# Joining the second graph's softmax totals with layer 0's totals in one 80-column product

## The chip, the cores and the metric

One core of a Trainium2 chip (trn2) runs the whole kernel in one launch. The metric is the device time of one execution in microseconds. Three runs of the kernel before are at hand; their median is what the changed kernel is held against. A separate execution was profiled, and every duration below comes from that one.

## The reference, cut to what matters

Sixty-four graphs of 256 nodes with 512 features pass through two graph layers, all in float32.

```python
# layer 0, for each graph: one attention of rank one, masked by adj
f = x @ fc_w.T + fc_b
logits = q(f) + k(f).T
a0 = softmax(leaky(logits + (1 - adj) * -1e9), axis=-1)
x1 = a0 @ f + x

# layer 1, for each graph: 8 heads of 64, weighted by adj
Q, K, V = x1 @ W_q + b_q, x1 @ W_k + b_k, x1 @ W_v + b_v
s = Q_h @ K_h.T / 8 + a[:, None] + c[None, :] + b_g + log(adj + 1e-9)
out = softmax(s, axis=-1) @ V_h + x1
```

Both softmaxes are computed without a maximum: the kernel forms the exponentials, uses them unnormalised in the products, and divides by their row totals later. The totals are what the change is about. `in_range` checks that no reciprocal of a total left a safe range; if one did, a general version at the end of the kernel would recompute everything.

## The kernel before, in words

The graphs are handled in 32 groups of two. The program is unrolled and its order is written out by hand: `step(d, a, f, n, check)` works on four groups at once. In step g, `f` is group g in its layer 0, `a` is group g-1 in its layer 1, `d` is group g-2, of which only the second graph's last part is left, and `n` is group g+1, whose inputs are being loaded. Short strings such as `D("attend:1 totals_1")` name the methods in the order in which they are issued; each engine's instructions are executed in that order. Step 0 has no `a`, steps 0 and 1 have no `d`, and the last step has no `n`, so it finishes group 30 by a tail of its own.

TensorE (PE) does the projections as seven block products each (`Product`, `Mixed`; L412), the scores `sc` (L843), the attention output `oT` (L883) and layer 0's mixing `y` (L667). VectorE (DVE) multiplies exponentials by the adjacency mask (`factor`, L863), adds them up (`both`, L870), and does the 32 x 32 transposes and the sums of block products. ScalarE (ACT) does the exponentials and copies out of PSUM.

A layer-1 total is made in four pieces. `parts` (L899, L900) transposes the summed exponentials in 32 x 32 blocks and reduces them, which leaves for each graph a tile `part` of 2 x 32 columns. `totals` (L910) multiplies it by `every`, a constant that adds over the four 32-row quarters of the partitions and spreads the sums; it does so in two products of 64 output partitions each, for even and odd heads. `ratios` (L925) takes reciprocals out of PSUM into `recip1`. `divide` (L983) multiplies the turned output `osb` by them, `complete` (L991) adds the residual and `store` sends it out.

Layer 0 has the same kind of total: `parts_0` (L613, L614) makes 16 columns in `part0`, `recip` (L621) multiplies them by `every`, four small ACT copies (L625) sort the result into `tot`, and a DVE reciprocal (L628) fills `recip0`.

The start of the step, where the change is, reads so before:

```python
A("scores:0")
D("attend:1 totals_1")
F("add_tiles")
A("scores:1 factor:0:0 factor:0:1 pv.sum_11 pv.p3 pv.p4")
D("ratios:1 turn:1")
F("parts_0")
A("factor:1:0 factor:1:1 pv.sum_10 both:0 both:1")
check()
F("mix:0 mix:1 ysum:0 recip")
D("divide:1 complete:1 store:1")
A("residual:1")
F("mix:2 mix:3 ysum:1 ysum:2 ysum:3")
```

`check()` does something in every fourth step only (steps 5, 9, 13, ... 29, and in 31): eight times it issues the six DVE instructions of `in_range` (L1030 to L1037). The second graph's totals of the group `d` were made ready (`parts:2`, `parts:3`) at the end of the step before.

Further on in the step, the features of layer 1 (`x`) are turned by DVE (`send`, L771), written to a DRAM buffer `xd` by the SP queue and read back turned (`fetch`, L789) as `x1T`. The third of four such pieces comes back by both the SP and the ACT queue (`fetch_by_both:0:1`). DVE's `xsum` (L375) forms block differences `t1b` of `x1T`, and PE's product `pq.p6` (`pq<-t1b,q_s`, L412) reads them.

PSUM has a pool of four banks that these products share (`bank`), and two pairs for the scores.

Of the kernel before, what the change touches and what calls it, by code (L numbers as in the profile page):

```python
# [10 lines left out]
F32 = mybir.dt.float32  # L11
I32 = mybir.dt.int32
AF = mybir.ActivationFunctionType
ALU = mybir.AluOpType
AX = mybir.AxisListType
ENGINES = {getattr(mybir.EngineType, e) for e in ("PE", "DVE", "Activation", "Pool", "SP")}

P = 128
# [7 lines left out]
def kernel(  # L26
# [64 lines left out]
    nc = tc.nc  # L91
    NB, N, D = x.shape
    NH = 8
    HD = D // NH
    B = 32
    RS = P // 4
    NC = D // P
# [3 lines left out]
    TOK = GP * N  # L101
# [14 lines left out]
            name=nc.get_next_instruction_name(), act_func_set_id=both[0], ins=[], outs=[]  # L116
# [43 lines left out]
    NR = 4  # L160
    recip0 = const.tile([P, NG, T], F32, tag="recip0", name="recip0")
    recip1 = const.tile([P, NR, GP, NC, N // B], F32, tag="recip1", name="recip1")

    def fast():
        main = ExitStack()
        with main:
            one = main.enter_context(tc.tile_pool(name="one", bufs=1))
            wts = main.enter_context(tc.tile_pool(name="wts", bufs=1))
            two = main.enter_context(tc.tile_pool(name="two", bufs=2))
# [9 lines left out]
            def bank(name):  # L179
                return ps.tile([P, 512], F32, tag="bank", name=name)  # L180
# [36 lines left out]
            every = const.tile([P, P], F32, tag="every", name="every")  # L217
            for q in range(P // B):
                for n in range(P // B):
                    rows = slice(q * B, (q + 1) * B)  # L220
# [299 lines left out]

            v_all = one.tile([P, T, D], F32, tag="v", name="v")

            class Group:


                def __init__(self, g):
                    self.g = g
# [80 lines left out]

                def parts_0(self):

                    turned = two.tile([P, TOK], F32, tag="xt", name=f"es0t_{self.g}")
                    self.part0 = one.tile([P, TOK // B], F32, tag="part0", name=f"part0_{self.g}")
                    nc.vector.transpose(turned, self.es0)  # L613
                    nc.vector.tensor_reduce(  # L614
                        self.part0, turned.rearrange("p (m c) -> p m c", c=B), AX.X, ALU.add
                    )

                def recip(self):

                    pt = bank(f"rc_{self.g}")[:, 0 : TOK // B]  # L620
                    nc.tensor.matmul(pt, lhsT=every, rhs=self.part0, start=True, stop=True)  # L621
                    tot = one.tile([P, T], F32, tag="tot0", name=f"tot0_{self.g}")
                    for q in range(P // B):
                        rows = slice(q * B, (q + 1) * B)
                        nc.scalar.copy(  # L625
                            tot[rows, :], pt[rows, :].rearrange("p (t q) -> p q t", q=P // B)[:, q]
                        )
                    nc.vector.reciprocal(recip0[:, self.g, :], tot)  # L628
# [263 lines left out]
                def parts(self, u):  # L892

                    g, (gr, hg), nb = self.g, divmod(u, 2), NC * N // B
                    if hg == 0:
                        self.part = two.tile([P, 2, nb], F32, tag="part", name=f"part_{g}_{gr}")
                    pool, tag = ((two, "osb"), (one, "e0"), (one, "e0"), (one, "adj"))[u]
                    turned = pool.tile([P, NC * N], F32, tag=tag, name=f"est_{g}_{u}")
                    nc.vector.transpose(turned, self.esum[u].rearrange("p a b i -> p (a b i)"))  # L899
                    nc.vector.tensor_reduce(  # L900
                        self.part[:, hg, :], turned.rearrange("p (m c) -> p m c", c=B),
                        AX.X, ALU.add,
                    )
# [19 lines left out]
                def ratios(self, gr):  # L923
                    self.rs = recip1[:, self.g % NR, gr]
                    nc.vector.reciprocal(self.rs.rearrange("p m b -> p (m b)"), self.tot)  # L925

                def sums_1(self, gr):

# [111 lines left out]
            def attention_and_layer_0(D, A, F, X, check):  # L1040

                A("scores:0")
                D("attend:1 totals_1")
                F("add_tiles")
                A("scores:1 factor:0:0 factor:0:1 pv.sum_11 pv.p3 pv.p4")
                D("ratios:1 turn:1")
                F("parts_0")
                A("factor:1:0 factor:1:1 pv.sum_10 both:0 both:1")
                check()
                F("mix:0 mix:1 ysum:0 recip")  # L1050
                D("divide:1 complete:1 store:1")
                A("residual:1")
                F("mix:2 mix:3 ysum:1 ysum:2 ysum:3")
                A("parts:0")
                F("pf.p1 pf.keep_1 pf.p2 pf.p6 pf.sum_00 begin send:0:0 fetch:0:0")
                A("turn_residual:1 parts:1")
                F("pf.p7 pf.p5")
                A("scores:2 attend:0 totals_0")
                F("pf.sum_11 send:1:1 fetch:1:1")
                A("factor:2:0 factor:2:1 turn:0")  # L1060
                F("pf.p3 pf.sum_01 send:0:1 pq.p1 pq.keep_1 copy:0 fetch_by_both:0:1")
                A("ratios:0 both:2")
                F("pf.p4 pf.sum_10 send:1:0")
                A("scores:3")
                F("fetch:1:0")
                A("factor:3:0")
                F("pk.p1 pk.keep_1 pv.p1 pv.keep_1")
# [16 lines left out]
            def step(d, a, f, n, check):  # L1084


                def of(group):
                    def issue(pieces):
                        for piece in pieces.split():
                            name, *args = piece.split(":")  # L1090
                            if group is None:
                                continue
                            target = group
                            if "." in name:
                                part, name = name.split(".")
                                target = getattr(group, part)
                            getattr(target, name)(*map(int, args))
                    return issue

                D, A, F, X = of(d), of(a), of(f), of(n)  # L1100
                X("load_adj")
                if a is not None:
                    attention_and_layer_0(D, A, F, X, check)
                else:
                    f.features_first()
                    F("pq.p1 pq.keep_1 copy:0 pk.p1 pk.keep_1 pv.p1 pv.keep_1")
                F("xsum:0 xsum:1 xsum:2 pq.p6 keys:2 keys:3 keys:0 keys:1")
                X("load_x")
                A("factor:3:1 both:3")
                F("pq.p7 pq.p2 pq.sum_00 xsum:3 pq.p5 pk.p6 pq.sum_11 pq.p3")  # L1110
                A("divide:0")
                X("dot_q:0 dot_q:1 dot_q:2 dot_q:3 spread")
                F("pq.p4 pq.sum_10 copy:1 copy:2")
                A("complete:0 store:0 parts:2")
                if n is None:
                    A("parts:3")
                F("pk.p7 pk.p5 pk.sum_11 residual:0")
                X("adjt")
                F("pk.p2 pk.sum_00")
                X("dot_k:0 dot_k:1")  # L1120
                F("pk.p3 pk.p4 pk.sum_10")
                X("dot_k:2 dot_k:3")
                F("turn_residual:0")
                if n is None:
                    A("attend:1 totals_1 ratios:1 turn:1 divide:1 complete:1 store:1")
                    F("residual:1 turn_residual:1")

                    F("pv.p2 scores:0 pv.p6 pv.sum_00 factor:0:0 factor:0:1 scores:1 both:0 pv.p7")
                    F("factor:1:0 factor:1:1 both:1 scores:2 pv.p5 sums_1:0 scores:3 pv.sum_11")
                    F("ratios_t:0 ratios_r:0 factor:2:0 factor:2:1 pv.p3 pv.p4 factor:3:0 pv.sum_10")  # L1130
                    F("factor:3:1 attend:0 finish:0 sums_of_e:1 attend:1")
                    F("ratios_t:1 ratios_r:1 finish:1")
                    check_ranges()()
                    return
                X("mask add_eps")
                F("pv.p2 pv.p6")
                X("weights:0")
                F("pv.p7 pv.p5")
                X("weights:1")
                F("pv.sum_00")  # L1140
                A("parts:3")

            with tc.manual_schedule(engines=ENGINES):
                f = Group(0)
# [8 lines left out]
                d, a, a_w = None, None, {}  # L1153
                for g in range(NG):
                    n = Group(g + 1) if g + 1 < NG else None

                    def check():

                        if d is not None and (d.g % NR == NR - 1 or d.g == NG - NR // 2 - 1):
                            in_range(d.g // NR * NR, d.g + 1, f"{d.g}")  # L1160
# [218 lines left out]
```

## Time and profile before

| what | value |
|---|---|
| median of 3 runs | 2327.16 us (2326.76 to 2327.59) |
| the profiled execution's own time | 2324.43 us |
| span of its first to its last instruction | 2322.6 us |
| PE busy | 2302.7 us, 99% of the span |
| DVE busy | 2092.7 us, 90% |
| ACT busy | 1071.0 us, 46% |
| granted TensorE clock, mean | 0.998 |

The profiled execution took 1.8 us more than its span and 2.7 us less than the median of the runs. A float32 product is carried out by PE in two passes, each with its own weight load (rows "PEld") and its own matmul record, so that the profile counts two or four records where the program has one or two products. The granted clock is full throughout, so durations of one row may be added.

### The profile page before, as it was taken

The numbers are of one execution on the slowest core, as the hardware profiler recorded it, in microseconds if no ns is written. First come the engines' busy times: TensorE is split into PE (matmuls) and PEld (weight loads), VectorE is DVE, ScalarE is ACT, GpSimd is POOL, SyncE is SP. The second block draws the span as 40 slices with busy tenths as digits, with TensorE's granted clock in tenths as the row PEclk, the third lists the DMA queues.
The fourth block names the chain that finished last, engine by engine and source line by source line (L and its number), as shares of the span: only waits on it lengthen the run. The fifth ranks groups of instructions, "written<-read, shape, count | busy, mean of one in ns | idle before, by whom it ended". The sixth has DMA issues, their size and how long they took to land.

```text
span 2322.6 us, 33706 instructions
## 1 busy us (share of the span) xinstructions
PE 2302.7 (99%) x12738; PEld 1906.0 (82%) x12738; DVE 2092.7 (90%) x3088; ACT 1071.0 (46%) x1865; POOL 122.0 (5%) x120
## 2 busy tenths in 40 slices
PE   9999999999999999999999999999999999999997
PEld 5888888888888888888888888888888888888885
DVE  6799889999899998999999999999999989999897
ACT  3544445444444444454444444444544445444443
POOL 0000000000000000000000000000000000000000
PEclk9999999999999999999999999999999999999999
DMA  4122323223322323232233223322222323323312
GB/s 132 48 59 72 78 75 67 64 66 84 79 73 56 68 73 78 73 69 60 69 80 84 64 61 67 80 78 73 64 60 73 78 74 68 64 64 85 79 46 38
DMA packets 517263, 163.84 MB, mean 71 GB/s; under 512 B 415188, under 2 KB 478696, under 8 KB 517096
## 3 DMA queue, kind: packets, MB, share of 16 engines
q1 hardware_dynamic: 505512, 156.25, 28.5%
q10 hardware_dynamic: 11584, 5.38, 0.8%
q8 instruction: 103, 1.69, 0.3%
q14 instruction: 64, 0.52, 0.1%
HBM read 95.43 MB, written 66.12 MB: 70 GB/s over the span
## 4 chain that ended last, share of the span: by engine, by line
PE 95%; DVE 2%; DMA 2%; issue 0%; ACT 0%; ACTq 0%; DVEq 0%
PE pv L412 17%; PE pq L412 16%; PE pk L412 16%; PE pf L412 16%; PE sc L843 10%; PE oT L883 10%; PE y L667 9%; DMA x1T<-xd 1%; DMA xd<-xt 1%; PE fp L696 1%; DVE t1b L375 0%; DMA fc_nat<-in_L_gnn_fc_w_dram 0%; PE tot L910 0%; DVE xt L771 0%; PE rc L621 0%
## 5 line engine op out<-in xcount | busy, mean ns | idle before, releaser
L863 DVE TENSOR_TENSOR e<-e,am 128x1024 f32<-128x1024 f32 x254 | 300.5, 1214 | 24.1 <-ACT e L857 24.1
L857 ACT ACTIVATE e<-sc,c 128x1024 f32<-128x1024 f32 x254 | 269.0, 1110 | 77.0 <-PE sc L843 73.5
L843 PE MATMUL sc<-qT,kT 64*128 64x256 f32 x2048 | 255.8, 389 | 0.4 <-ACT e L857 0.4
L883 PE MATMUL oT<-e,v 128*64 128x256 f32 x2032 | 233.4, 382 | 0.0
L495 POOL TENSOR_TENSOR pf_s<-pf_s,x 128x512 f32<-128x512 f32 x93 | 118.5, 1274 | 2118.7 <-ACT pf_s L494 1673.4
L843 PEld LDWEIGHTS sc<-qT,kT 64*128 64x128 f32 x2048 | 187.2, 186 | 51.5 <-issue 31.5
L667 PE MATMUL y<-e,x 128*128 128x256 f32 x992 | 226.1, 382 | 0.0
L883 PEld LDWEIGHTS oT<-e,v 128*64 128x64 f32 x2032 | 140.2, 137 | 85.4 <-issue 21.3
L432 ACT ACTIVATE pq_s<-pq,cols 128x256 f32<-128x256 f32 x192 | 80.5, 470 | 279.1 <-PE pq L412 279.1
L667 PEld LDWEIGHTS y<-e,x 128*128 128x128 f32 x992 | 186.1, 190 | 24.0
L494 ACT ACTIVATE pf_s<-pf,recip 128x256 f32<-128x256 f32 x186 | 77.9, 470 | 197.6 <-PE pf L412 197.6
L900 DVE TENSOR_REDUCE part<-est 128x32 f32<-128x1024 f32 x124 | 151.3, 1220 | 4.3
L899 DVE STREAM_TRANSPOSE est<-es 128x1024 f32<-128x1024 f32 x124 | 152.2, 1227 | 0.0
L870 DVE TENSOR_TENSOR es<-e,e 128x1024 f32<-128x1024 f32 x126 | 149.3, 1205 | 1.1
L673 ACT COPY yT<-y 128x512 f32<-128x512 f32 x124 | 72.6, 586 | 131.5 <-PE y L667 130.8
L890 ACT COPY oTs<-oT 128x512 f32<-128x512 f32 x128 | 75.0, 586 | 119.1 <-PE oT L883 98.4
L429 ACT COPY pk_s<-pk 128x512 f32<-128x512 f32 x96 | 56.3, 586 | 151.9 <-PE pk L412 151.9
L412 PE MATMUL pk<-x1T,wk 128*128 128x256 f32 x512 | 124.2, 385 | 0.0
L412 PE MATMUL pk<-t1b,wk 128*128 128x256 f32 x512 | 121.1, 379 | 0.4 <-DVE kT L443 0.4
L412 PE MATMUL pv<-wv,t1b_c 128*128 128x256 f32 x512 | 121.1, 379 | 0.0
L412 PE MATMUL pv<-wv,t1b 128*128 128x256 f32 x512 | 121.1, 379 | 0.0
L412 PE MATMUL pq<-x1T,wq 128*128 128x256 f32 x512 | 121.0, 379 | 0.0
(180 smaller groups left out, 4474.7 us busy)
## 6 DMA issues: line engine op xcount, KB each, us to landing
x<-in_x_dram SPq DMA_DIRECT2D x32, 1024.0 KB, 5.1
out_dram<-osb SPq DMA_DIRECT2D x254, 128.0 KB, 3.3
xd<-xt SPq DMA_DIRECT2D x124, 256.0 KB, 2.0
x1T<-xd SPq DMA_DIRECT2D x434, 64.0 KB, 1.9
adj<-in_adj_dram SPq DMA_DIRECT2D x128, 128.0 KB, 3.5
qrow<-q SPq DMA_DIRECT2D x31, 256.0 KB, 3.9
x1T<-xd ACTq DMA_DIRECT2D x62, 64.0 KB, 2.4
fc_nat<-in_L_gnn_fc_w_dram ACTq DMA_DIRECT2D x4, 256.0 KB, 3.8
```

What stands on the lines that cost most here:

```text
L412: nc.tensor.matmul(o, lhsT=lk[:, ts(m, P)] if len(lk.shape) == 2 else lk[:, m], rhs=rk, start=(start and m == 0 and k == 0), stop=(m == 1 ...
L432: nc.scalar.activation(dst[:, m], src[:, m], AF.Identity, bias=self.bias[:, 2 * o + m : 2 * o + m + 1],)
L494: nc.scalar.mul(s[:, m], src[:, m], self.recip[:, TPG * k + m : TPG * k + m + 1])
L495: nc.gpsimd.tensor_tensor(s, s, self.out(o, k), ALU.add)
L667: nc.tensor.matmul(y[:, ts(gr, N)], lhsT=self.x[:, gr * TPG + j, ts(c, P)], rhs=self.e0[:, j, gr, :], start=(gr == 0 and j == 0), stop=(gr ...
L843: nc.tensor.matmul(sc[:, par, pr, :], lhsT=self.kT[rows, 2 * hg + pr, ts(t, P)], rhs=self.qT[rows, 2 * hg + pr, ts(gr, N)], start=True, st ...
L857: nc.scalar.activation(e, sc, AF.Exp, bias=self.c[:, t : t + 1], scale=SCALE)
L863: nc.vector.tensor_tensor(ef, ef, self.am[:, jc, u // 2, :].unsqueeze(1).to_broadcast([P, 4, N]), ALU.mult,)
L870: nc.vector.tensor_tensor(self.esum[u], self.e[u, 0], self.e[u, 1], ALU.add)
L883: nc.tensor.matmul(oT[par * HD : (par + 1) * HD, pr, :], lhsT=self.v[:, gr * TPG + jc, ts(h, HD)], rhs=self.e[2 * gr + hg, jc][:, par, pr, :],
L899: nc.vector.transpose(turned, self.esum[u].rearrange("p a b i -> p (a b i)"))
L900: nc.vector.tensor_reduce(self.part[:, hg, :], turned.rearrange("p (m c) -> p m c", c=B), AX.X, ALU.add,)
```

## The change

`totals_1` and its two products of 2 x 16 columns are taken out of the step. `parts` now puts the second graph's 64 columns into the first part of a tile of 80 columns (`part_all`), and the younger group's `parts_0` writes layer 0's 16 columns behind them. `recip` multiplies all 80 columns by the full `every` in one product; its first 64 columns are handed to the older group (`all_sums`), the last 16 serve layer 0 as before. `ratios:1`, one reciprocal on 128 partitions, is replaced by `ratios_of_all`: two reciprocals on 64 partitions each, since even and odd heads now lie in different columns. It stands behind `recip`, just ahead of `divide:1`. `check()` moves behind `store:1`, so that it sees the new reciprocals. In step 1, which has no older group, `recip` keeps its 16 columns; the first graph's totals (`totals_0`, `ratios:0`) and the tail of the last step stay as they were.

```diff
+            ALL = 2 * NC * N // B + TOK // B
+
             class Group:
+                older = None
...
                     turned = two.tile([P, TOK], F32, tag="xt", name=f"es0t_{self.g}")
-                    self.part0 = one.tile([P, TOK // B], F32, tag="part0", name=f"part0_{self.g}")
+                    if self.older is None:
+                        self.parts_all = two.tile(
+                            [P, ALL], F32, tag="part", name=f"part0_{self.g}"
+                        )
+                    else:
+                        self.parts_all = self.older.part_all
                     nc.vector.transpose(turned, self.es0)
                     nc.vector.tensor_reduce(
-                        self.part0, turned.rearrange("p (m c) -> p m c", c=B), AX.X, ALU.add
+                        self.parts_all[:, ALL - TOK // B : ALL], turned.rearrange("p (m c) -> p m c", c=B), AX.X, ALU.add
                     )
...
-                    pt = bank(f"rc_{self.g}")[:, 0 : TOK // B]
-                    nc.tensor.matmul(pt, lhsT=every, rhs=self.part0, start=True, stop=True)
+                    lo = ALL - TOK // B
+                    first = lo if self.older is None else 0
+                    all_sums = bank(f"rc_{self.g}")[:, 0:ALL]
+                    nc.tensor.matmul(
+                        all_sums[:, first:ALL], lhsT=every, rhs=self.parts_all[:, first:ALL],
+                        start=True, stop=True,
+                    )
+                    if self.older is not None:
+                        self.older.all_sums = all_sums[:, 0:lo]
+                    pt = all_sums[:, lo:ALL]
...
-                        self.part = two.tile([P, 2, nb], F32, tag="part", name=f"part_{g}_{gr}")
+                        self.part_all = two.tile([P, ALL], F32, tag="part", name=f"part_{g}_{gr}")
+                        self.part = self.part_all[:, 0 : 2 * nb].rearrange("p (a m) -> p a m", a=2)
...
+                def ratios_of_all(self):
+                    self.rs = recip1[:, self.g % NR, 1]
+                    sums = self.all_sums.rearrange("p (a b m) -> p b a m", a=2, b=2)
+                    for par in range(2):
+                        rows = slice(par * HD, (par + 1) * HD)
+                        nc.vector.reciprocal(
+                            self.rs[rows].rearrange("p (a n) b -> p a (n b)", a=2), sums[rows, par]
+                        )
...
-                D("attend:1 totals_1")
+                D("attend:1")
...
-                D("ratios:1 turn:1")
+                D("turn:1")
                 F("parts_0")
                 A("factor:1:0 factor:1:1 pv.sum_10 both:0 both:1")
+                F("mix:0 mix:1 ysum:0 recip")
+                D("ratios_of_all divide:1 complete:1 store:1")
                 check()
-                F("mix:0 mix:1 ysum:0 recip")
-                D("divide:1 complete:1 store:1")
                 A("residual:1")
...
+                f.older = d
```

## The prediction

> **What bounds the kernel now.** I read the engines' shares first, then the chain that ended last, then PE's own waits.
>
> ```profile
> span 2322.6 us, 33706 instructions
> ...
> PE 2302.7 (99%) x12738; PEld 1906.0 (82%) x12738; DVE 2092.7 (90%) x3088; ACT 1071.0 (46%) x1865; POOL 122.0 (5%) x120
> ...
> PE 95%; DVE 2%; DMA 2%; issue 0%; ACT 0%; ACTq 0%; DVEq 0%
> ```
>
> PE's queue is the bound: 95% of the chain is PE after PE. So a step takes what PE's instructions take (71.16 us from one `rc` product to the next in 24 of the 30 intervals), and other engines count only where PE waits for them. PE's waits say where that is:
>
> ```profile
> PE pq L412 <- DVE t1b L375: 3.3, 6, 1.3
> ```
>
> Six waits, 3.34 us in all, and nothing else recurs. They are in steps 3, 4, 11, 18, 19 and 26, the intervals that are longer than 71.16 us. One of them, in time (start, length, instruction):
>
> ```profile
> 1327.75 0.69 DVE L375 TENSOR_TENSOR t1b<-x1T 128x512 f32<-128x512 f32 x1 [0.90 <-DMA x1T<-xd]
> 1328.47 0.69 DVE L375 TENSOR_TENSOR t1b<-x1T,t1b 128x512 f32<-128x512 f32 x1
> 1329.22 0.92 PE L412 MATMUL pq<-t1b,q_s 128*128 128x256 f32 x3 [0.35 <-DVE t1b L375]
> ```
>
> DVE waits for the third read-back of `x1T`, PE for DVE's second difference. In an ordinary step the first difference starts 26.93 us after `rc` and PE needs nothing before 28.89; as PE starts 0.06 us after the second difference ends (28.34), 0.49 us are spare.
>
> **What the Trainium skill says.** "TensorEngine Tiling (Array Packing)", Key Properties: changing the tiling mode drains TensorE. The trace agrees: from `pf` (whole array) to the scores (64 rows) the starts are 309 ns apart where whole-array passes are 216 ns apart. "TensorE: Matmul & The Clock Gate", LDWEIGHTS (loading the stationary operand): a load takes time by its columns, 128 / 1.2 = 107 ns; here back-to-back loads of 128 columns start 110 ns apart. "VectorE: DVE Perf Modes", Two Vector instructions with no wait between them: an instruction that starts in another quarter of the partitions than the one before is held until that has finished. The trace agrees: the four copies of L974 on different quarters start one duration plus 13 ns apart, while L925 and its successor overlap (332 ns long, 0.25 us from start to start). "Runtime: NRT & Kernel Launch", Instruction fetch mechanics: instructions come by DMA in blocks of 16 KiB, 256 of them. The trace has 103 such packets on queue 8, one for every 256 PE records, 0.9 to 1.9 us long.
>
> **PE: the removed product.** The second graph's totals in two steps, and the scores where they follow a plain product:
>
> ```profile
> 1219.54 0.26 PE L910 MATMUL tot<-part,every 128*64 128x32 f32 x4
> 1219.72 0.92 PE L843 MATMUL sc<-qT,kT 64*128 64x256 f32 x6
> ```
>
> ```profile
> 1169.16 0.81 PE L412 MATMUL pf<-fcT,tb 128*128 128x256 f32 x3
> 1169.90 0.70 PE L843 MATMUL sc<-qT,kT 64*128 64x256 f32 x4
> ```
>
> Record by record, the last `oT` pass before the totals starts at 1219.326, the first score at 1219.723: 209 + 35 + 152 = 396 ns. Without totals, `oT` (64 columns) meets the scores (64 rows) directly. No place in the steady steps shows this change of mode; its nearest rows are `pf` to `sc`, 309 ns, and the reverse `sc` to `oT`, 306 ns. The first pair of scores then takes 320 ns in both cases. I take 306: **90 ns saved in each of 30 steps (2 to 31), 2.7 us.** Bounds: at best the drain and the first pair's extra 104 ns vanish with the totals, 396 + 320 - 432 = 284 ns, 8.5 us; at worst the totals' slot is all drain anyhow and nothing is saved.
>
> **PE: the wider product.**
>
> ```profile
> 1228.66 0.29 PE L621 MATMUL rc<-part,every 128*128 128x16 f32 x2
> 1228.80 0.68 PE L667 MATMUL y<-e,x 128*128 128x256 f32 x2
> ```
>
> A pass of 256 columns takes 216 ns, 0.84 ns a column: 16 columns stream in 13 ns, 80 in 67 ns. But the two `rc` passes and the next `y` pass start their work 110 ns apart, as each waits for its weights, loaded while the pass before streams. 67 ns fit into 110. **Cost 0**; if the columns came on top, 64 x 0.84 x 2 = 108 ns a step, 3.2 us. Less than nothing is excluded: no weight load goes away here.
>
> **DVE.** One reciprocal of 332 ns leaves its old place ahead of `turn:1`. Nothing is gained: DVE then waits longer for `yT`. Two go in after the reciprocal of L628:
>
> ```profile
> 1300.64 0.69 DVE L350 TENSOR_TENSOR tb<-yT 128x512 f32<-128x512 f32 x1 [0.80 <-ACT yT L673]
> 1301.25 0.17 DVE L628 RECIPROCAL recip<-tot 128x4 f32<-128x4 f32 x1
> 1301.34 1.19 DVE L983 TENSOR_TENSOR osb<-osb,recip 128x1024 f32<-128x1024 f32 x1
> 1302.57 1.22 DVE L991 TENSOR_TENSOR osb<-osb,xb 128x1024 f32<-128x1024 f32 x1
> 1304.32 0.69 DVE L350 TENSOR_TENSOR tb<-yT,tb 128x512 f32<-128x512 f32 x1 [0.53 <-ACT yT L673]
> ```
>
> They lie on different quarters, so neither overlaps: 2 x 0.345 = 0.69 us (cover: the 0.53 us wait in the last line, which leaves 0.16 us). Behind are `ysum`, `parts:0`, the sums of `pf` and the sends on SP. The next wait of DVE, 0.90 us for POOL's `pf_s` ahead of the second sum of `pf`, swallows the rest. **Cost 0 in a step without a check.** The reciprocals add no wait either: L628, just ahead of them, already waits for ACT's copies of the same PSUM bank.
>
> **The moved check, eight steps.** Its six instructions take 1.62 us. Before, 0.80 us of that ran while DVE would have waited for `yT`, and the 0.53 us wait took most of the rest; the sum `ysum:1` came only 0.12 us late. Now the check stands after `complete`: `ysum:1` starts 0.16 + 1.62 = 1.78 us late, at 6.28 us after `rc`, and ends at 6.96; PE's `pf.p6` reads it as weights and starts at 7.13, with its 110 ns load this just fits. Then the delay goes down the queue: 1.78 - 0.90 (wait for POOL) = 0.88, less 0.14 idle ahead of the third sum: the third `send` is **0.74 us late**, and on SP and ACT its two-queue `fetch` behind it. `pf.p4`'s wait (0.50) and ACT's `e` (0.67) bring DVE itself back. The read-back then lands about 27.4 us after `rc` instead of 26.6; the first difference can start up to 27.42 before PE waits. Cost about 0 without a fetch of instructions in the way (between 0 and 0.3 us each, 0 to 1.8 us), and the whole 0.74 us where one makes the read-back late already.
>
> **Which steps these are.** All six waits are steps where a block of PE instructions comes in 22.8 to 25.6 us after `rc`, that is 282 to 318 records into the step (places counted in multiples of 256); 268 and 334 brought none. A step has 802 PE records, so the place moves back by 34 a step. The totals take 8 away, and perhaps a wait instruction: 793 or 794, a shift of 25 or 26. Counting on, blocks fall on 282 to 318 in steps 4, 5, 14, 15 (near its edge), 25 or 24, with 24 or 26 doubtful: about six again, so I leave their 3.34 us as they are (2 to 6 us possible). Steps 5 and 25 are check steps: **2 x 0.74 = 1.5 us lost.**
>
> **Other edits.** PSUM: a freed bank goes to the next tile in order of release. One tile less per step gives `y` of chunk 0 the bank of the first `oT`, long copied; the bank of `rc`, now freed by `ratios_of_all` (about 2.2 us after `rc`), goes to `pf.p2` at 5.4 us. Cover 3 us, cost 0. `parts` writes into a wider tile at the same durations (L900, 1220 ns). The `rc` product waits for `parts_0` as before; `parts:3` is done 11 us earlier. ACT, POOL and the stores keep their order; `store:1` comes 0.7 us later on SP in plain steps and SP then waits for `send` anyway.
>
> **Sum.** -2.7 + 0 + 0 + 1.5 = -1.2 us: 2324.4 becomes 2323.2 in the profiled execution. This stood 2.7 us under the median; held against the median, 2327.2 - 1.2 = **2326.0 us**.
>
> **Rivals.**
> A, *forecast*: PE saves its 90 ns and the checks give half back: 2322.4 to 2330.5. Chance 0.81, within 0.2% (4.7 us, about what a measurement of this kernel can tell from no change).
> B, *slower*: DVE's lateness reaches PE. If the third send is late by 0.74 us in all eight check steps and the read-back's margin is already used up, and the slower drift gives seven fetches at the price of steps 3 and 4 (1.0 us each on average): -2.7 + 8 x 0.74 + (7.2 - 3.3) = +7.1, 2334.3 us. It decides once the read-back lands later than 27.4 us in ordinary steps too. For it: 0.49 us spare is little. Against: waits of 0.90, 0.50 and 0.67 us lie between. Chance 0.12.
> C, *faster*: no drain between `oT` and the scores (284 ns a step, -8.5 us) and no loss at the checks: 2318.7 us. Against: `sc` to `oT` shows the drain. Chance 0.07.
> D, *it does not do what it says*: 80 columns stream on top, +3.2 us: 2329.2 us, inside the range and within A's chance.
>
> **Numbers.** The low end is A with no loss at the checks and two microseconds fewer of fetch waits (2322.4); the high end has D and one more fetch of instructions at step 4's price, 1.3 us (2330.5). Outside lie C and B.
>
> **What would show it.** Right: `oT` to `sc` starts about 306 ns apart, `rc` to `y` unchanged at 140 ns, L350's 0.53 us wait nearly gone, steps of 71.07 us, PE waits for `t1b` near 4 to 5 us in all, in steps 4, 5, 14, 15, 25. Wrong: waits of PE in most check steps, a new releaser in PE's waits, or `rc` to `y` longer by about 100 ns.

## The result, and the profile after

The changed kernel takes **2331.47 us** (median of 20 runs), the kernel before 2326.61 us (median of 20): a ratio of 1.0021, 95% interval 1.0015 to 1.0028, that is 4.9 us more. The forecast was 2326.0 us, within 0.2% of the kernel before, with a range that ended at 2330.5 us.

The shares and the chain of waits of the changed kernel (busy time, share of the span, instructions; then shares of the chain that ended last):

```profile
span 2329.5 us, 33496 instructions
...
PE 2304.3 (99%) x12618; PEld 1896.3 (81%) x12618; DVE 2114.3 (91%) x3118; ACT 1070.9 (46%) x1865; POOL 124.3 (5%) x120
...
PE 86%; DVE 8%; DMA 3%; issue 1%; ACT 0%; SPq 0%; ACTq 0%; POOL 0%; DVEq 0%
```

PE has 120 matmul records fewer, yet its part of the chain fell from 95% to 86%; DVE's rose from 2% to 8%. PE's waits (what waited, for what, us in total, times, longest):

```profile
PE pq L412 <- DVE t1b L375: 10.3, 12, 1.3
```

Before it was 3.3 us in six waits. Step by step, from one `rc` product to the next, the plain steps became shorter, from 71.162 to 71.075 us, and the steps with a check became longer, to 72.24 us (steps 9, 13, 17, 21 and 29, within 0.03 us of each other).

| where, profiled executions | us |
|---|---|
| 30 steps, each 87 ns shorter | -2.6 |
| the check steps 5 to 29, beyond 71.08 us | +8.7 |
| waits in other steps: 4.4 after, 5.0 before | -0.6 |
| start-up, until the first `rc` product | +1.3 |
| from the last `rc` product to the end | +0.1 |
| sum (spans: 2329.5 - 2322.6) | +6.9 |

The start-up is not of the change: with the same start the kernels below reach their first `rc` product between 87.4 and 91.0 us. The medians, 4.9 us apart, agree with the first three rows (+5.5) within a microsecond. The eighth check, in step 31, hides in the row before the last: PE waits 0.73 us there too and its last wait ends 1.0 us later, but what follows that wait took 6.8 us instead of 7.7. It takes 6.7 to 7.0 us in every run with the change and 7.8 in experiment 2, which is without it; the cause stays open.

This is check step 9 in the timeline, on DVE and POOL (start, length, instruction, idle time before it); `rc` starts at 659.29:

```profile
665.48 0.16 DVE L1068 TENSOR_TENSOR okp<-okp,okp 128x1 f32<-128x1 f32 x1
665.56 0.68 DVE L350 TENSOR_TENSOR tb<-yT,tb 128x512 f32<-128x512 f32 x1
666.16 1.76 DVE L350 TENSOR_TENSOR tb<-yT 128x512 f32<-128x512 f32 x1
667.85 0.68 DVE L350 TENSOR_TENSOR tb<-yT,tb 128x512 f32<-128x512 f32 x1
...
665.82 1.56 POOL L495 TENSOR_TENSOR pf_s<-pf_s,x 128x512 f32<-128x512 f32 x1 [62.90 <-ACT pf_s L494]
```

The check's last instruction is followed by the three `ysum`. The second of them takes 1.76 us where its neighbours take 0.68: it starts while POOL adds `x` to `pf_s`, and ends only after that. Before, POOL's add, at the same 6.5 us after `rc`, lay over a transpose and a reduction and met no such instruction. Check step 17 of the kernel before (DVE, then POOL; `rc` starts at 1228.66):

```profile
1235.09 1.24 DVE L899 STREAM_TRANSPOSE est<-es 128x1024 f32<-128x1024 f32 x1
...
1235.18 1.28 POOL L495 TENSOR_TENSOR pf_s<-pf_s,x 128x512 f32<-128x512 f32 x1 [62.98 <-DVE tb L350]
```

The rest of the way to PE, in step 9 of the changed kernel:

```profile
684.58 0.85 ACTq L808 DMA_DIRECT2D x1T<-xd  x2
685.48 2.12 ACT L876 ACTIVATE e<-sc,c 128x1024 f32<-128x1024 f32 x2 [3.01 <-PE sc L862]
686.62 1.23 DVE L882 TENSOR_TENSOR e<-e,am 128x1024 f32<-128x1024 f32 x1 [1.25 <-ACT e L876]
687.79 0.69 DVE L375 TENSOR_TENSOR t1b<-x1T 128x512 f32<-128x512 f32 x1
688.52 0.69 DVE L375 TENSOR_TENSOR t1b<-x1T,t1b 128x512 f32<-128x512 f32 x1
689.27 1.56 PE L412 MATMUL pq<-t1b,q_s 128*128 128x256 f32 x6 [0.88 <-DVE t1b L375]
```

The third send is late, so the ACT queue issues its half of the read-back late (25.30 us after `rc` instead of 23.74). Behind it in the same queue stand the exponentials of `scores:3`: they start at 26.2 us, though the last of these scores ended at 25.4. Behind these stands `factor:3:0`, and behind that, without idle time, the block differences, and PE.

### The profile page after: what moved, and what is told of

Same layout as the page of the kernel before. It is cut to its first block, busy times and chain, and to the rows that moved or that the text cites. A ratio compares the mean times of both kernels' runs of the same rounds, so it can differ in the third digit from the quotient of the medians.

```text
span 2329.5 us, 33496 instructions
## 1 busy us (share of the span) xinstructions
PE 2304.3 (99%) x12618; PEld 1896.3 (81%) x12618; DVE 2114.3 (91%) x3118; ACT 1070.9 (46%) x1865; POOL 124.3 (5%) x120
## 4 chain that ended last, share of the span: by engine, by line
PE 86%; DVE 8%; DMA 3%; issue 1%; ACT 0%; SPq 0%; ACTq 0%; POOL 0%; DVEq 0%
PE pv L412 16%; PE pq L412 16%; PE pk L412 16%; PE pf L412 12%; PE sc L862 9%; PE oT L902 8%; PE y L686 8%; DMA xd<-xt 2%; DMA x1T<-xd 1%; DVE x L501 1%; DVE est L919 1%; DVE xt L790 1%; DVE t1b L375 1%; DVE tb L350 1%; PE fp L715 1%
## 5 line engine op out<-in xcount | busy, mean ns | idle before, releaser
L412 PE MATMUL pq<-t1b,q_s 128*128 128x256 f32 x512 | 117.1, 382 | 10.4 <-DVE t1b L375 10.3
```

The source lines that it names most:

```text
L412: nc.tensor.matmul(o, lhsT=lk[:, ts(m, P)] if len(lk.shape) == 2 else lk[:, m], rhs=rk, start=(start and m == 0 and k == 0), stop=(m == 1 ...
```

## The experiments

**1. Without the checks.** 

> The changed kernel without the range checks inside the steps (left out: the check of all reciprocals but the last two groups'). Theory 1 (the moved check makes the third send late, and PE waits about 0.86 us in each of the eight check steps): those waits go, what is left is PE's 0.083 us a step and the fetch steps; about 2324 us, 2.5 to 3 us under the kernel before, and the interval of a check step without a fetch of instructions is 71.08 us. Theory 2 (the two held reciprocals or the joint product are what costs): the time stays near 2331 us.

```diff
                 D("ratios_of_all divide:1 complete:1 store:1")
-                check()
```

Measured 2322.8 us, ratio to before 0.9986 (0.9979 to 0.9992). The intervals of steps 9, 13, 17, 21 and 29 are 71.08 us. So the product and the two reciprocals save what they were to save; everything that made the change slower hangs on the check.

**2. The kernel before, with the check moved.** 

> The kernel before with the one edit that check() stands behind store:1; totals and reciprocals as they were. Theory 1: the loss of the changed kernel appears without its product: PE waits 0.7 to 0.9 us in each check step, 1.0 to 1.2 us longer intervals, about 2326.6 + 8 x 1.1 = 2335 us. Theory 2: no change, 2326 to 2327 us.

```diff
-                check()
                 F("mix:0 mix:1 ysum:0 recip")
                 D("divide:1 complete:1 store:1")
+                check()
```

Measured 2327.7 us, ratio 1.0006 (0.9998 to 1.0014): a miss for theory 1 as I had put it. The timeline of its step 9 (DVE, then POOL) shows why it is informative:

```profile
668.54 0.68 DVE L350 TENSOR_TENSOR tb<-yT 128x512 f32<-128x512 f32 x1
669.14 1.76 DVE L350 TENSOR_TENSOR tb<-yT,tb 128x512 f32<-128x512 f32 x1
...
668.94 1.40 POOL L495 TENSOR_TENSOR pf_s<-pf_s,x 128x512 f32<-128x512 f32 x1 [62.99 <-ACT pf_s L494]
```

The collision is here too, with the third `ysum` instead of the second, 1.08 us again. But without the two late reciprocals the whole queue is 0.76 us earlier: the first late `ysum` starts 5.51 us after `rc` instead of 6.27, and the third send ends at 22.35 instead of 23.23. That is just at the edge: PE's wait is 0.01 to 0.02 us in four check steps (intervals of 71.44 to 71.45 us, 0.28 more than a plain step), 0.09 in step 9 and 0.66 in step 13, where a block of instructions came at 19.7 us. Moved check and collision together cost little; the reciprocals' 0.7 us on top are what is too much.

Step 5 has no wait at all. Its check is one instruction shorter (there is no earlier check to join), so that the third `ysum` starts at 6.51 us and POOL's add at 6.52. There the `ysum` keeps its 0.69 us, and it is the add that takes 1.82 instead of 1.27 us: the one that starts second is held.

**3. The check behind the third send.** 

> The changed kernel with check() behind the third send and its fetch instead of behind store:1. Theory 1: the third send is on time again; the 1.62 us of the check are taken up by DVE's later idle time (0.50 us ahead of the fourth sum, 0.67 us ahead of factor:3:0), which leaves about 0.45 us of the 0.49 us to spare; no wait of PE in plain check steps: about 2324 us. Theory 2: 2331 us as before the move.

```diff
                 D("ratios_of_all divide:1 complete:1 store:1")
-                check()
...
                 F("pf.p3 pf.sum_01 send:0:1 pq.p1 pq.keep_1 copy:0 fetch_by_both:0:1")
+                check()
                 A("ratios:0 both:2")
```

Measured 2323.7 us, ratio 0.9989 (0.9982 to 0.9995): faster than both kernels, and by the two ratios about 7.4 us under the changed one. The third send ends at 21.68 us in every step, and steps 9, 13, 17, 21 and 29 take 71.08 us. PE's waits are those of steps 4, 5, 14, 15 and 24, where blocks of instructions come, and of step 19:

```profile
PE pq L412 <- DVE t1b L375: 3.8, 6, 1.0
```

**4. The check behind the three `ysum`.** 

> The changed kernel with check() behind ysum:1, ysum:2 and ysum:3 instead of ahead of them; the check is as long and still ahead of the third send. Theory 1a (of the 1.55 us that the third send is late, 1.08 us come from ysum:2 running beside POOL's add and taking 1.76 instead of 0.68 us): the ysums keep their 0.68 us, the third send is about 0.75 us late, PE waits 0 to 0.3 us in plain check steps: 2324 to 2327 us. Theory 1b (the check's own length is all that counts, wherever it stands ahead of the third send): waits as in the changed kernel, about 2331 us.

```diff
-                check()
                 A("residual:1")
                 F("mix:2 mix:3 ysum:1 ysum:2 ysum:3")
+                check()
```

Measured 2332.4 us, ratio 1.0026 (1.0016 to 1.0036). The number is what theory 1b said, but the timeline of step 9 (DVE, then POOL) is not:

```profile
664.49 0.69 DVE L350 TENSOR_TENSOR tb<-yT,tb 128x512 f32<-128x512 f32 x1
665.09 0.17 DVE L1061 TENSOR_SCALAR ok<-recip 128x16 f32<-128x16 f32 x1
665.30 1.17 DVE L1062 SCALAR_TENSOR_TENSOR ok<-recip,ok 128x16 f32<-128x16 f32 x1
...
665.16 1.26 POOL L495 TENSOR_TENSOR pf_s<-pf_s,x 128x512 f32<-128x512 f32 x1 [62.90 <-ACT pf_s L494]
```

The `ysum` keep their 0.68 us, as 1a said. Now it is an instruction of the check itself, on 16 elements, that meets POOL's add: 1.17 us instead of 0.17. Both theories were put too narrowly. A third, 1c: any DVE instruction with two inputs in SBUF that starts during POOL's add waits for the add's end, whichever it is. The next two runs test that.

**5. Without POOL's first add.** 

> The changed kernel, check() where the change puts it, but without POOL's first add of pf_s in each step (left out: the residual x of one block of layer 0, in every group). Theory 1c (a DVE instruction with two SBUF inputs that meets POOL's add is held until the add ends; in the check steps that costs ysum:2 1.08 us): ysum:2 takes 0.68 us in the check steps too, the second sum of pf starts near 15.7 us after rc instead of 16.7, the third send ends near 22.2 instead of 23.2, PE waits 0 to 0.1 us in plain check steps: 2323 to 2325.5 us. Theory 1b (the check's length is all): as the changed kernel, about 2331 us.

```diff
-                    nc.gpsimd.tensor_tensor(s, s, self.out(o, k), ALU.add)
+                    if n != 1:
+                        nc.gpsimd.tensor_tensor(s, s, self.out(o, k), ALU.add)
```

Measured 2324.75 us, ratio 0.9996 (0.9987 to 1.0004). The first two `ysum` in its check step 9, after the same check at the same place:

```profile
665.40 0.68 DVE L350 TENSOR_TENSOR tb<-yT,tb 128x512 f32<-128x512 f32 x1
666.01 0.68 DVE L350 TENSOR_TENSOR tb<-yT 128x512 f32<-128x512 f32 x1
```

The second `ysum` takes 0.68 us, the second sum of `pf` starts 15.64 us after `rc` (changed kernel: 16.71), the third send ends at 22.15 (23.23), and the plain check steps take 71.17 us instead of 72.24.

**6. The check where POOL's adds meet nothing.** 

> The changed kernel with check() between turn_residual:1 and parts:1, still ahead of the second and third send, at a place where POOL's adds (6.5 to 7.8, 10.0 to 11.3 and from 13.4 us after rc) lie over transposes, a sum out of PSUM or the idle time after the check. Nothing is left out. Theory 1c: no instruction of the check is held, the second sum starts near 15.7, the third send ends near 22.2, PE waits 0 to 0.1 us in plain check steps: 2323 to 2325.5 us. Theory 1b: 2331 us.

```diff
-                check()
                 A("residual:1")
...
-                A("turn_residual:1 parts:1")
+                A("turn_residual:1")
+                check()
+                A("parts:1")
```

Measured 2325.3 us, ratio 0.9997 (0.9988 to 1.0005), with nothing left out. The six instructions keep their lengths and the next POOL add falls on a transpose (DVE, then POOL):

```profile
671.74 0.17 DVE L1062 SCALAR_TENSOR_TENSOR ok<-recip,ok 128x16 f32<-128x16 f32 x1
...
673.16 1.24 DVE L919 STREAM_TRANSPOSE est<-es 128x1024 f32<-128x1024 f32 x1
...
673.35 1.28 POOL L495 TENSOR_TENSOR pf_s<-pf_s,x 128x512 f32<-128x512 f32 x1 [2.13 <-ACT pf_s L494]
```

The second sum starts at 15.64, the third send ends at 22.16, four of the plain check steps take 71.17 to 71.18 us. In step 17 PE waits 1.20 us. There the write of the second piece to `xd`, issued at 17.28 us, landed at 21.64 instead of 19.3; SP, which waits for it, issued the third write 1.3 us late, and the third fetch followed at 25.6 us instead of 24.2. A block of PE's instructions came at 19.2 us, during that second write; that it is the cause is likely, but no run shows it. The check is as long as in the changed kernel and still ahead of two sends: 1b falls, 1c stands.

**7. Blocks of instructions 128 records earlier.** 

> The kernel with check() behind the third send, with 38 instead of 6 products in the warm-up at the start of the program: 128 PE records more ahead of the steps, so that the blocks of 256 PE instructions are fetched 128 records earlier in the step. Start-up gets up to 7 us longer; only the steps in which PE waits for t1b are looked at. If a block of instructions that arrives during the third read-back makes PE wait: the waits leave steps 4, 5, 14, 15 and 24 and come in 9, 10, 19, 20, 29 and perhaps 30. If the waits belong to those groups' data or to other transfers, they stay in 4, 5, 14, 15, 24.

```diff
-                for n in range(6):
+                for n in range(38):
                     nc.tensor.matmul(warm[:, 0:P], lhsT=ident, rhs=ident, start=True, stop=True)
```

One run: 2328.6 us, of which 6.6 us are the longer start-up. PE waits in steps 9, 10, 19, 20 and 29 (0.44, 1.45, 1.34, 0.10 and 0.17 us) and in none of 4, 5, 14, 15 and 24. Apart from step 19, the waits follow the blocks of PE instructions. In step 19 a fetch issued 0.9 us late is there in every kernel, whatever the place of PE's blocks; that part has another cause, which stays open.

## Why the prediction was wrong

**PE's removed product: right.** From `oT` to the scores, the timeline of the changed kernel:

```profile
649.82 0.60 PE L902 MATMUL oT<-e,v 128*64 128x256 f32 x4
650.36 1.35 PE L862 MATMUL sc<-qT,kT 64*128 64x256 f32 x10
```

The last `oT` pass and the first score start 309 ns apart (forecast 306, before 396); with the change of mode in place rival C is out. A plain step is 87 ns shorter, against 90 forecast: 2.6 us in 30 steps.

**The wider product: right, with a wrong sign to look for.** The second `rc` pass starts 69 ns after the first instead of 28, and `y` 112 ns after that as before. My "`rc` to `y` unchanged at 140 ns" therefore failed, 181 ns, and yet nothing was lost: the 87 ns saved at `oT` reach the step in full. The weight load of that `y` pass starts 111 or 112 ns after `rc` and the next `y` pass 439 ns after it, in both kernels; the 41 ns lie in between and moved neither. Rival D is out.

**The reciprocals in plain steps: right.** `ysum:1` starts at 4.64 us instead of 4.50 (forecast 0.16 us late), the second and third sums of `pf` are on time, and no plain step lost anything.

**The steps with blocks of instructions: right.** Waits came in 4, 5, 14, 15, 24 and 25, as counted, 5 and 25 dearer than the other check steps (intervals of 72.36 and 72.65 us). A seventh wait, 0.26 us, came in step 19 without a block. The prediction had put step 19's wait down to the block that came there before, but the fetch is late by the same 0.9 us in both kernels; so one of its six waits was probably read wrongly, without harm to the sum. Outside the check steps these waits cost 4.4 us, before 5.0.

**The moved check: the step that failed.** "Then the delay goes down the queue" began right (`ysum:1` at 6.27 us, forecast 6.28) and then went wrong in three terms.

- *The delay is 2.85 us, not 1.78: the term that decided.* I costed `ysum:2` at its row's 0.68 us wherever it stands, and said of POOL only that it keeps its order. The missing 1.08 us are the collision with POOL's add, which starts about 6.5 us after `rc`, set by PE and ACT; moving DVE's work by 1.8 us put a two-input instruction under it. Less the 0.90 us wait for POOL and 0.14 us of idle time, the third send should be 1.81 us late; it is 1.55 (forecast 0.74), as a short idle time ahead of other instructions is used up too. Experiment 5 is the case that the prediction had in mind, with the collision gone: the third send is 0.47 us late (forecast 0.74), and a plain check step costs 0.10 us, so that "about 0" would have held. The Trainium skill has the rule, on a page that the prediction does not draw on: "SBUF — State Buffer", Who interferes with whom, says that a DVE instruction with two SBUF inputs contends with a GpSimd instruction that reads SBUF, that one of the two waits for the other's whole instruction, and that a DVE instruction with one SBUF input (outside the modes that use both of DVE's ports) does not contend. The runs agree in all three. In the changed kernel and experiments 2 and 4, 22 two-input instructions started during an add, and all took 1.0 to 1.1 us longer (0.68 became 1.76 and 0.17 became 1.17 us). In all runs, transposes under the same add kept their 1.20 to 1.24 us, reductions their 1.22, and the sums of `pf`, with one input in PSUM, their 0.48.
- *The spare time is 0.39 us, not 0.8.* I let the read-back land at 27.4 us where 27.42 was allowed, as if only the data mattered. But the late send holds ACT's queue, and the chain of exponentials, `factor:3:0` and differences follows the fetch at a fixed 3.18 us (25.30 to 28.48 after, 23.74 to 26.92 before; likewise 24.22 to 27.41 in experiments 5 and 6). That it is the queue and not the data is read from the timeline; no run separates the two. So what can be late is the difference itself, and the prediction's own 0.49 us is the most that is spare. The intervals show still less: a difference 0.49 us late costs 0.10 us (experiments 5 and 6), 0.68 us late 0.28 (experiment 2), 1.56 us late 1.17 (the changed kernel), always 0.39 less.
- *A wait costs more than its record.* The waits of 0.86 us stand in steps that are 1.17 us longer, the waits of 0.01 to 0.02 us of experiment 2 in steps 0.28 us longer. PE's weight load has to wait as well: in a plain step that of `pq.p6` starts 0.21 us ahead of its matmul, in step 17 of experiment 2 together with it, and so it is no longer hidden. The interval shows the price, the wait does not.

With these, a plain check step costs 1.17 us instead of "about 0". The seven check steps to 29 lost 8.7 us where I had 1.5 in two of them (1.0 of the 8.7 is the block of step 5, which costs as much without a check, in experiment 1), and -2.6 + 8.7 - 0.6 = +5.5 us stands where the sum said -1.2. It is rival B's place, DVE's lateness reaching PE in the check steps, but not B's point of decision: ordinary steps kept their margin, and the fetches of instructions did not become dearer.

## What to carry to other kernels

When instructions are moved on one engine, look not only at who waits for them but at what will then run beside them: here a 1.8 us shift put a two-input DVE instruction under POOL's add, and the add's remaining length came on top. Spare time is to be measured along every queue that the late event holds (a DMA issue on ACT's queue holds the exponentials behind it), and it is shared by all edits: of the reciprocals, the check and the collision, any one taken away, the rest cost a plain check step at most 0.4 us, where all three cost 1.17. A rare piece of work belongs behind the last transfer that the bounding engine waits for; there the same check cost nothing in the plain check steps, and the joined product was worth its 2.6 us.

## What the runs showed of the hardware that I had not expected

A DVE instruction on 16 elements took 1.17 us instead of 0.17 because POOL's add had started 0.14 us before it; in the changed kernel POOL's add was stretched too (1.56 us instead of 1.27), since it started while the `ysum` before was still running. Which of the two loses goes by which starts first: where the `ysum` was 0.01 us ahead, in step 5 of experiment 2, only the add became longer. Where a block of 16 KiB of PE's instructions arrived during the third piece's write or read-back of 256 KB, the first difference came up to 2.1 us late (experiment 7, step 10), and which steps are hit is decided by the number of PE instructions per step: 8 records fewer moved the hits to other steps, 128 more at the start moved them again.
